# Four graph layers on one core: halves for the first and last group, a 64x64 turn of the adjacency, and later places for its forms and for the layernorms of layer 2

## The chip, the cores and the metric

The kernel runs on one core of a Trainium2 chip. A core has five engines that take their instructions in order, each from its own queue: TensorE (PE, with its weight loads shown apart as PEld), VectorE (DVE), ScalarE (ACT), GpSimd (POOL) and SyncE (SP), which only issues DMAs here. The metric is the device time of one execution in microseconds (us). The version before takes 2535.03 us, the median of three runs from 2534.58 to 2535.87. All values are fp32.

## The reference

x holds 128 batches of 64 nodes with 256 features; adj is one 64x64 matrix for all batches. There are four layers, each with a layernorm and a ReLU in front and a residual add behind.

```python
# layer 0: two graph convolutions, then LSTMs over windows of 1 to 4 nodes
h = relu(einsum('ts,bsh->bth', adj, x @ Wg0 + bg0))
h = relu(einsum('ts,bsh->bth', adj, h @ Wg1 + bg1))
for p in range(1, 5):
    ...
# layer 1: attention with 4 heads, masked where adj == 0
# layer 2: normalized adjacency and a net with two batchnorms
A_norm = A + eye(n)
deg = sum(A_norm, 0) + sum(A_norm, 1) - diagonal(A_norm)
dinv = rsqrt(deg)
A_hat = A_norm * dinv[:, None] * dinv[None, :]
x = einsum('nm,bmd->bnd', A_hat, features).reshape(-1, d)
h = relu(batchnorm(x @ W1.T + b1))
out = batchnorm(h @ W2.T + b2)
# layer 3: three times support = x @ W, then (adj * adj) @ support, with ReLU after the first two
# around each of them:
h = maximum(layernorm(x), 0.0)
x = x + layer(h)
```

The adjacency is thus needed in several forms: transposed for the graph convolution (`adj2`), its row sums for the biases, squared (`w2s`), as a mask, and normalized with both degrees (`ah2`).

## The kernel before, in words

The 8192 tokens (128 batches x 64 nodes) are worked in NG = 16 groups of GN = 512 tokens. A group is four tiles (GT) of 128 tokens on the partitions, two batches in a tile, so the adjacency stands twice on the partitions, once for each half of 64. All results of TensorE go through eight PSUM banks in rotation (`bank`). The order of the instructions on each engine comes from a scheduler; `tc.issue_after(ins)` tells it to put what follows behind `ins`. An engine stands still at an instruction whose input isn't ready, whatever is behind it.

Helpers: `ln_scale` (L83 to L98) makes the scale and shift of a layernorm for four tiles: four bn_stats on DVE (L91), four bn_aggr (L93), an add (L94), a power of -0.5 on POOL (L95) and a product on DVE (L97). `ln_apply` (L102) is four ACT activations, one for each tile. `mix` (L122 to L147) multiplies the tokens with a 64x64 adjacency form in 64 small matmuls (L134) into two banks and copies the two banks to SBUF (L146, in layer 3 also L143), by the engines that it is given. `seven` (L153 to L180) combines seven products to a 2x2 block product, with adds on DVE (L165, L166, L174, L177) and POOL (L169), and hands its blocks to `ends_in` (L197), which puts the ReLU of layer 3 on ACT, from a bank (L202) for the first block and in place (L204) for the other three.

Layer 0: the adjacency arrives twice from memory on ACT's queue. `abd` (L270) holds it as two 64x64 blocks on the diagonal of a cleared 128x128 tile, `arow` (L272) holds it in two stacks of rows. One 128x128 transpose turns `abd` (L275), and two 64x64 copies (L280) put the diagonal blocks in `adj2`; they are called from within the layernorm of group 0, ahead of L97. `adjacency_forms` (L285 to L300) makes the row sums by a matmul (L290), the mask, `w2s` and a full copy of the turned tile; `normalized_adjacency` (L302 to L323) makes `ah2`, with degrees from three reductions, a power on POOL (L317), another 128x128 transpose (L320) and two products (L323). Both are called at group 1, behind its layernorm. The loop at L419 runs over g and calls in this order: `first_mix(g)`, `second_weights(g-2)` (L407, adds L412, ReLU on ACT L415), `second_mix(g-1)` with both copies on ACT, `first_weights(g)` (L383, adds L391 on DVE, ReLU L392 on POOL). The x tiles come by SP's queue (L58), the weights of the convolution by ACT's (L328).

Layer 2: `activated` (L664) is the layernorm of a group, `mixed` (L670) its mix with `ah2`, `hidden` (L674) sixteen matmuls into four banks (L680), each bank read by ACT (L686, the eviction with the bias) and by DVE (bn_stats, L689). The loop at L882 calls for each g the layernorm and the mix of g+1, then hidden(g). All layernorms there may start as soon as the attention is done (`after_attention`), as far as buffers and queues allow. After the first batchnorm (`bn_finish`, L862) the loop at L918 applies it (L921), multiplies with the second weight matrix, eight matmuls a group into two banks (L928), evicts the banks on ACT (L937) and then takes their statistics on DVE (L940). A second `bn_finish` follows; nothing of layer 3 can start before it.

Layer 3: `normalize` (L947) applies the second batchnorm, one feature half on ACT (L951) and one on DVE (L954). `to_residual` (L957) turns the result by eight transposes (L964) in two banks, and adds each bank to x (L968). `start` (L971) is the layernorm and first mix of a group, `first_weights` (L981, products L991) ends in the ReLUs of `ends_in`, `second_mix` (L1006) mixes them in two rounds, `second_weights` (L1027) and `third_weights` (L1072) follow, `last_mix` (L1093) is the last adjacency product, and `finish` (L1100) adds two banks to x (L1103) and sends 512 KB out (L1104).

Of the kernel before, what the change touches and what calls it, by code (L numbers as in the profile page):

```python
# [8 lines left out]
F32 = mybir.dt.float32  # L9
AF = mybir.ActivationFunctionType  # L10
# [4 lines left out]
P = 128  # L15
# [23 lines left out]
def adj_preln_kernel(ctx: ExitStack, tc: tile.TileContext, x_in, adj, vec, bg0, bg1,  # L39
# [31 lines left out]
    adjT = const.tile([P, P], F32, tag="adjT", name="adjT")  # L71
# [11 lines left out]
    def ln_scale(src, between=None):  # L83


        st = lnp.tile([P, GT, 6], F32, tag="st", name="st")
        mv = lnp.tile([P, GT, 2], F32, tag="mv", name="mv")
        rstd = lnp.tile([P, GT], F32, tag="rstd", name="rstd")
        nmr = lnp.tile([P, GT], F32, tag="nmr", name="nmr")
        for t in range(GT):  # L90
            nc.vector.bn_stats(st[:, t, :], src[:, t, :])  # L91
        for t in range(GT):
            nc.vector.bn_aggr(mv[:, t, :], st[:, t, :])  # L93
        nc.vector.tensor_scalar(rstd, mv[:, :, 1], LN_EPS, None, ALU.add)  # L94
        nc.gpsimd.tensor_tensor(out=rstd, in0=rstd, in1=mhalf, op=ALU.pow)  # L95
        with tc.issue_after(between().ins) if between else nullcontext():
            last = nc.vector.scalar_tensor_tensor(nmr, mv[:, :, 0], -1.0, rstd, ALU.mult, ALU.mult)  # L97
        return rstd, nmr, last.ins  # L98

    def ln_apply(src, dst, rstd, nmr):  # L100
        for t in range(GT):
            nc.scalar.activation(  # L102
                dst[:, t, :], src[:, t, :], AF.Relu,
                bias=nmr[:, t : t + 1], scale=rstd[:, t : t + 1],
            )
# [91 lines left out]
    def ends_in(out, func):  # L197


        def end(m, n, ps):  # L200
            if ps is not None:
                nc.scalar.activation(out[m][n], ps, func)  # L202
            elif func != AF.Copy:
                nc.scalar.activation(out[m][n], out[m][n], func)  # L204

        return end
# [45 lines left out]
    with tc.tile_pool(name="lw", bufs=5) as lw:  # L252
# [6 lines left out]
        with tc.tile_pool(name="gw", bufs=1) as gw, tc.tile_pool(name="gcn", bufs=2) as gp, \  # L259
                tc.tile_pool(name="setup", bufs=1) as sp:  # L260

            for g in range(2):
                load_x(xs[g], g)
            abd = sp.tile([P, P], F32, tag="abd", name="abd")
            nc.vector.memset(abd, 0.0)
            arow = sp.tile([P, NODES], F32, tag="arow", name="arow")
            ones = sp.tile([NODES, P], F32, tag="ones", name="ones")
            nc.vector.memset(ones, 1.0)
            for b in range(2):
                nc.scalar.dma_start(out=abd[b * 64 : b * 64 + 64, b * 64 : b * 64 + 64], in_=adj)  # L270
            for b in range(2):
                nc.scalar.dma_start(out=arow[b * 64 : b * 64 + 64, :], in_=adj)  # L272
            nc.sync.dma_start(out=vecs, in_=vec)
            pt = bank((P, P))
            nc.tensor.transpose(pt, abd, ident)  # L275

            def diagonal_blocks():
                for b in range(2):
                    blk = slice(b * 64, b * 64 + 64)
                    last = nc.vector.tensor_copy(adj2[blk, :], pt[blk, blk])  # L280
                return last

            rstd0, nmr0, first_ln = ln_scale(xs[0], diagonal_blocks)

            def adjacency_forms():  # L285
                nc.vector.tensor_tensor(
                    lbias, vecs[:, V_BIH : V_BIH + 32], vecs[:, V_BHH : V_BHH + 32], ALU.add
                )
# [5 lines left out]
                for c in range(2):  # L294
                    nc.vector.tensor_scalar(
                        rb1[:, c, 0, :], rsrow, bcol[:, c : c + 1], None, ALU.mult
                    )
                nc.vector.tensor_scalar(mask, arow, 0.0, NEG, ALU.is_equal, ALU.mult)
                nc.vector.tensor_tensor(w2s, adj2, adj2, ALU.mult)
                nc.vector.tensor_copy(adjT, pt)  # L300

            def normalized_adjacency():  # L302
                an = sp.tile([P, P], F32, tag="an", name="an")
                anT = sp.tile([P, P], F32, tag="anT", name="anT")
                dg = sp.tile([P, P], F32, tag="dg", name="dg")
# [3 lines left out]
                nc.vector.tensor_tensor(an, abd, ident, ALU.add)  # L309
                nc.vector.tensor_tensor(anT, adjT, ident, ALU.add)  # L310
                nc.vector.tensor_tensor(dg, an, ident, ALU.mult)
# [7 lines left out]
                pt2 = bank((P, P))  # L319
                nc.tensor.transpose(pt2, an, ident)  # L320
                for b in range(2):
                    blk = slice(b * 64, b * 64 + 64)
                    nc.vector.tensor_scalar(ah2[blk, :], pt2[blk, blk], dinv[blk, :], None, ALU.mult)  # L323
# [20 lines left out]
            first_copied, middle_copied, second_ln = None, None, None  # L344

            def first_mix(g):
                nonlocal first_copied, middle_copied, second_ln
                h = gp.tile([P, GT, D], F32, tag="h", name="h")
                if g == 0:
                    ln_apply(xs[0], h, rstd0, nmr0)  # L350
                elif g == 1:

                    with tc.issue_after(first_copied):
                        rstd, nmr, second_ln = ln_scale(xs[1])
                    ln_apply(xs[1], h, rstd, nmr)
                    with tc.issue_after(second_ln):
                        adjacency_forms()
                        normalized_adjacency()
                else:
# [5 lines left out]
                    with tc.issue_after(second_ln):  # L365
                        ln_relu(x, h)
                m0 = gp.tile([P, 2, GN], F32, tag="m0", name="m0")
                copied = mix(h, adj2, 2, m0, (on_vector, on_vector))
                if g == 0:
                    first_copied = copied  # L370
                if g == NG // 2:
                    middle_copied = copied
# [22 lines left out]
            def second_mix(h1):  # L395
                m1 = gp.tile([P, 2, GN], F32, tag="m1", name="m1")
                mix(h1, adj2, 2, m1, (on_scalar, on_scalar))
# [21 lines left out]
            for g in range(NG + 2):  # L419
# [4 lines left out]
                m1 = second_mix(h1) if h1 is not None else None  # L424
# [249 lines left out]
    def hidden(g, w1, ms=range(4)):  # L674
# [10 lines left out]
        for m, ps in zip(ms, pss):  # L685
# [3 lines left out]
            nc.vector.bn_stats(st1[:, m, g, :], ps)  # L689


    with tc.tile_pool(name="att", bufs=2, reuse_waits="tile") as ap_:
# [113 lines left out]
        for g in range(NG + 1):  # L806
# [31 lines left out]
            else:  # L838
                hidden(0, w1, range(2, 4))
# [41 lines left out]

    for g in range(1, NG):  # L882
        if g + 1 < NG:
            with tc.issue_after(after_attention):
# [3 lines left out]
        hidden(g, w1)  # L888
# [29 lines left out]
    for g in range(NG):  # L918
# [7 lines left out]
        for c in range(4):  # L926
            for m in range(2):
                nc.tensor.matmul(  # L928
                    pss[m], lhsT=w2[:, c, m * P : (m + 1) * P], rhs=a[:, c, :],
                    start=(c == 0), stop=(c == 3),  # L930
                )
# [4 lines left out]
        for m in range(2):  # L936
            nc.scalar.activation(  # L937
                o[:, m, :], pss[m], AF.Identity, bias=vecs[:, V_B2 + m : V_B2 + m + 1]
            )
            nc.vector.bn_stats(st2[:, m, g, :], pss[m])  # L940
# [6 lines left out]
    def normalize(g):  # L947

        o = outs[g // 2][:, 2 * (g % 2) : 2 * (g % 2) + 2, :]
# [7 lines left out]
    def to_residual(g):  # L957
        o = outs[g // 2][:, 2 * (g % 2) : 2 * (g % 2) + 2, :]
        for k in range(2):
# [11 lines left out]
    def start(g, behind=None):  # L971
# [4 lines left out]
        with tc.issue_after(behind) if behind else nullcontext():  # L976
            ln_relu(xs[g], h)
# [3 lines left out]
    def first_weights(a, room):  # L981
# [6 lines left out]
        def product(w, b):  # L988
# [13 lines left out]
            blocks, ends_in(blocks, AF.Relu),  # L1002
# [97 lines left out]
    def finish(g, pss):  # L1100
        for q in range(2):
# [21 lines left out]
    normalize(0)  # L1123
    to_residual(0)
    a = start(0)
# [77 lines left out]
```

## Time and profile before

| | us |
|---|---|
| median of three runs | 2535.03 |
| the profiled execution, its own time | 2534.2 |
| its span | 2532.4 |
| TensorE busy in it | 2481.1 |
| DVE busy | 1462.8 |
| ACT busy | 1132.3 |
| POOL busy | 418.5 |

The mean clock granted to TensorE is 0.993 of full speed. The profile is one execution; its times are microseconds from the start of the span. A timeline row gives start and duration, engine and line, operation, output and inputs, shape and count, and in brackets how long the engine was idle before it and what ended that. A row of waits gives the waiting engine and line, what it waited for, and then the total, the number of times and the longest. A row of windows gives for a stretch of time the busy time of each engine (with instructions begun), the granted clock, the DMA engines' busy share and GB/s.

Three rows of DMA issues, with the time from issue to landing at the end:

```profile
x<-in_x SPq DMA_DIRECT2D x28, 512.0 KB, 6.2
out<-x SPq DMA_DIRECT2D x16, 512.0 KB, 2.9
...
wg<-in_wg ACTq DMA_DIRECT2D x2, 256.0 KB, 4.0
```

The end of the execution, in the timeline:

```profile
2525.75 1.34 PE L1093 MATMUL ps<-arena,w2s 64*64 64x256 f32 x16
...
2527.13 1.29 DVE L1103 TENSOR_TENSOR x<-x,ps 128x512 f32<-128x512 f32 x2 [0.85 <-PE ps L1093]
2528.44 0.37 SPq L1104 DMA_DIRECT2D out<-x  x1
```

The last two adds begin when the last matmuls are done, and the span ends when the last 512 KB have been sent.

### The profile page before, as it was taken

What the parts mean: (1) busy time and instruction counts of PE and PEld (TensorE: products, weight loads), DVE (VectorE), ACT (ScalarE), POOL (GpSimd) and SP (SyncE); (2) the same over time, 40 slices, a digit from 0 to 9 for tenths busy, and PEclk for the clock granted to TensorE, in tenths of its full rate; (3) what the DMA queues carried; (4) which work ended last, traced back from release to release, by engine and by line L of the source; (5) the groups of instructions that cost most, each with busy time, mean ns of one, the idle gap of its engine ahead of it and who ended that gap; (6) DMA issues with size and microseconds to landing.
All of it is one profiled execution on the core that took longest, in us unless ns stands there. A gap on an engine that the chain in (4) does not pass through costs nothing.

```text
span 2532.4 us, 46818 instructions
## 1 busy us (share of the span) xinstructions
PE 2481.1 (98%) x20184; PEld 2046.5 (81%) x20184; DVE 1462.8 (58%) x2606; ACT 1132.3 (45%) x1982; POOL 418.5 (17%) x350
## 2 busy tenths in 40 slices
PE   7999999999999999999999989998999999999999
PEld 5668888889999998888766654445898888888888
DVE  6647876666566575565566675415455454554544
ACT  4547754444444443444555464653333333333332
POOL 3422211111111111111122220003101101111110
PEclk9999999999999999999999999998999999999999
DMA  3200000001000000000300000010000000000000
GB/s 113 102 1 1 1 17 1 1 1 34 1 1 1 1 1 1 1 13 1 101 2 2 2 19 1 1 58 1 9 10 10 18 10 10 18 10 10 18 9 18
DMA packets 30206, 39.66 MB, mean 16 GB/s; under 512 B 1712, under 2 KB 26416, under 8 KB 30000
## 3 DMA queue, kind: packets, MB, share of 16 engines
q1 hardware_dynamic: 29136, 36.09, 4.2%
q8 instruction: 158, 2.59, 0.4%
q10 hardware_dynamic: 864, 0.59, 0.1%
q14 instruction: 48, 0.39, 0.1%
HBM read 28.29 MB, written 8.39 MB: 14 GB/s over the span
## 4 chain that ended last, share of the span: by engine, by line
PE 90%; DVE 4%; ACT 2%; POOL 2%; issue 1%; DMA 0%; DVEq 0%; POOLq 0%; ACTq 0%
PE ps L461 40%; PE ps L1027 15%; PE ps L1072 8%; PE ps L707 4%; PE ps L928 4%; PE ps L134 4%; PE ps L680 3%; PE ps L991 3%; PE ps L723 2%; PE ps L383 2%; PE ps L407 2%; POOL rstd L95 1%; DVE st L91 1%; ACT arena L204 1%; PE ps L784 1%
## 5 line engine op out<-in xcount | busy, mean ns | idle before, releaser
L461 PE MATMUL ps<-diff,s 128*128 128x256 f32 (+1 forms) x1824 | 393.5, 371 | 0.9 <-DVE diff L577 0.9
L1027 PE MATMUL ps<-arena 128*128 128x256 f32 x1792 | 392.7, 381 | 0.8 <-DVE arena L186 0.8
L1027 PEld LDWEIGHTS ps<-arena 128*128 128x128 f32 x1792 | 337.8, 190 | 55.1 <-issue 10.4
L461 PEld LDWEIGHTS ps<-diff,s 128*128 128x128 f32 x1824 | 345.9, 190 | 33.8 <-issue 1.6
L475 ACT ACTIVATE gates<-gates,lbias 128x512 f32<-128x512 f32 (+5 forms) x426 | 244.1, 620 | 203.6 <-DVE gates L174 146.3
L169 POOL TENSOR_TENSOR gates<-p 128x512 f32<-128x512 f32 (+1 forms) x115 | 148.8, 1294 | 885.1 <-DVE p L166 834.0
L461 PE MATMUL ps<-h,w 128*128 128x256 f32 (+1 forms) x1028 | 241.2, 371 | 1.6 <-ACT p L162 1.6
L461 PE MATMUL ps<-diff,w 128*128 128x256 f32 (+1 forms) x1040 | 238.7, 370 | 0.0
L461 PEld LDWEIGHTS ps<-diff,w 128*128 128x128 f32 x1040 | 197.4, 190 | 18.2
L461 PEld LDWEIGHTS ps<-h,w 128*128 128x128 f32 x1028 | 194.6, 190 | 20.9 <-ACT p L162 2.0
L475 ACT ACTIVATE gates<-ps,lbias 128x256 f32<-128x256 f32 (+3 forms) x213 | 91.8, 477 | 247.0 <-PE ps L461 246.9
L204 ACT ACTIVATE arena<-arena 128x512 f32<-128x512 f32 x144 | 88.1, 628 | 192.4 <-POOL arena L169 103.3
L169 POOL TENSOR_TENSOR arena<-arena 128x512 f32<-128x512 f32 x64 | 73.2, 1144 | 537.9 <-DVE arena L166 537.9
L1072 PE MATMUL ps<-arena 128*128 128x128 f32 x1280 | 149.9, 276 | 0.0
L1072 PEld LDWEIGHTS ps<-arena 128*128 128x128 f32 x1280 | 145.6, 192 | 1.3 <-issue 0.2
L174 DVE TENSOR_TENSOR gates<-p,ps 128x512 f32<-128x512 f32 (+1 forms) x115 | 76.5, 665 | 119.8 <-PE ps L461 119.8
L174 DVE TENSOR_TENSOR arena<-arena,ps 128x512 f32<-128x512 f32 x64 | 39.7, 621 | 149.4 <-PE ps L1027 84.7
L680 PE MATMUL ps<-arena,w 128*128 128x512 f32 x256 | 115.8, 605 | 1.4 <-DVE arena L146 1.3
L461 PE MATMUL ps<-state,w 128*128 128x256 f32 (+1 forms) x512 | 116.1, 370 | 0.9 <-ACT p L162 0.8
L461 PE MATMUL ps<-state,s 128*128 128x256 f32 (+1 forms) x512 | 115.8, 369 | 0.0
L177 DVE TENSOR_TENSOR gates<-p,ps 128x512 f32<-128x512 f32 (+1 forms) x115 | 76.7, 667 | 64.8 <-PE ps L461 64.1
L707 PE MATMUL ps<-hT,w 128*128 128x512 f32 x256 | 112.8, 593 | 0.0
(184 smaller groups left out, 3884.2 us busy)
## 6 DMA issues: line engine op xcount, KB each, us to landing
x<-in_x SPq DMA_DIRECT2D x28, 512.0 KB, 6.2
out<-x SPq DMA_DIRECT2D x16, 512.0 KB, 2.9
w<-in_wih SPq DMA_DIRECT2D x4, 1024.0 KB, 7.6
w<-in_whh SPq DMA_DIRECT2D x3, 1024.0 KB, 5.0
arena<-in_l3w SPq DMA_DIRECT2D x3, 1024.0 KB, 5.0
w<-in_wqkv SPq DMA_DIRECT2D x1, 768.0 KB, 4.4
wg<-in_wg ACTq DMA_DIRECT2D x2, 256.0 KB, 4.0
w<-in_w1t SPq DMA_DIRECT2D x1, 512.0 KB, 3.8
```

The costliest lines, as they stand in the source:

```text
L134: nc.tensor.matmul(pss[b][half * 64 : half * 64 + 64, c, t, :], lhsT=src[rows, t, col : col + 64], rhs=a2[rows, :], start=True, stop=True,)
L169: nc.gpsimd.tensor_tensor(out=out[1][1], in0=p1, in1=p5, op=ALU.add)
L174: nc.vector.tensor_tensor(out[0][1], p1, ps[1], ALU.add)
L177: nc.vector.tensor_tensor(out[1][0], p1, ps[3], ALU.add)
L204: nc.scalar.activation(out[m][n], out[m][n], func)
L461: nc.tensor.matmul(ps[:, r], lhsT=wc[:, j, :], rhs=bc, start=first and r == 0 and c == 0, stop=True, skip_group_check=True,)
L475: nc.scalar.activation(o, ps, func, bias=lbias[:, col : col + 1])
L680: nc.tensor.matmul(ps, lhsT=w1[:, c, m * P : (m + 1) * P], rhs=a[:, 2 + c, :], start=(c == 0), stop=(c == 1),)
L707: nc.tensor.matmul(ps, lhsT=wqk[:, c, col : col + P], rhs=hT[:, c, :], start=(c == 0), stop=(c == 1),)
L928: nc.tensor.matmul(pss[m], lhsT=w2[:, c, m * P : (m + 1) * P], rhs=a[:, c, :], start=(c == 0), stop=(c == 3),)
L1027: nc.tensor.matmul(ps[:, r, :], lhsT=w[:, c, col : col + P], rhs=b[:, c, :], start=first and r == 0 and c == 0, stop=c == 1, skip_group_ch ...
L1072: nc.tensor.matmul(ps[:, t, :], lhsT=w[:, c, t * P : (t + 1) * P], rhs=b[:, c, :], start=first and t == 0 and c == 0, stop=c == 3, skip_gr ...
```

## The change

1. `abd`, its clearing, its two DMAs and `adjT` are gone. The adjacency is turned by two 64x64 matmuls of `arow` with the identity (`by_batch`), one for each half of the partitions, into one 128x64 bank, and one copy makes `adj2`. The DMAs of `arow` are the first on ACT's queue. x of group 0 is loaded in two halves, and its layernorm is made and applied in two halves of two tiles (`ln_scale` and `ln_apply` with n = 2).
2. Of group 0's mix the first bank is copied by ACT, the second by DVE. The layernorm of group 1 is put behind that of group 0, not behind the copies.
3. The row sums stay at group 1. The other forms and the normalized adjacency, now 128x64 each, are made at group NG // 4 = 4, behind the copies of its mix.
4. The second mix of the last group is copied by ACT and DVE.
5. In layer 2 the layernorm of group g+1 is put behind the statistics of hidden(g-3), for the first groups behind the attention and hidden(0).
6. In the second half of layer 2 the statistics of a bank are called ahead of its eviction, and the last group's eight matmuls fill one bank after the other.
7. Group 0 of layer 3 is normalized, turned, added, and put through its layernorm by halves.
8. Of the four ReLUs of a group in layer 3's first product, that of block (1, 0) is on DVE.
9. The last group is added in four parts and sent out in two halves.

```diff
-            abd = sp.tile([P, P], F32, tag="abd", name="abd")
-            nc.vector.memset(abd, 0.0)
-            for b in range(2):
-                nc.scalar.dma_start(out=abd[b * 64 : b * 64 + 64, b * 64 : b * 64 + 64], in_=adj)
+            for k in range(2):
+                nc.sync.dma_start(
+                    out=xs[0][:, 2 * k : 2 * k + 2, :], in_=x_view[:, 2 * k : 2 * k + 2, :]
+                )
...
-            pt = bank((P, P))
-            nc.tensor.transpose(pt, abd, ident)
+            def by_batch(ps, rows):
                 for b in range(2):
                     blk = slice(b * 64, b * 64 + 64)
-                    last = nc.vector.tensor_copy(adj2[blk, :], pt[blk, blk])
+                    nc.tensor.matmul(
+                        ps[blk, :], lhsT=rows[blk, :], rhs=ident[blk, blk], start=True, stop=True
+                    )
+            pt = bank((P, NODES))
+            by_batch(pt, arow)
+            lns = [
+                ln_scale(xs[0][:, 0:2], lambda: nc.vector.tensor_copy(adj2, pt), 2),
+                ln_scale(xs[0][:, 2:4], None, 2),
+            ]
+            first_ln = lns[1][2]
...
-                nc.vector.tensor_tensor(an, abd, ident, ALU.add)
-                nc.vector.tensor_tensor(anT, adjT, ident, ALU.add)
-                nc.vector.tensor_tensor(dg, an, ident, ALU.mult)
+                nc.vector.tensor_tensor(eye, ident[:, 0:64], ident[:, 64:128], ALU.add)
+                nc.vector.tensor_tensor(an, arow, eye, ALU.add)
+                nc.vector.tensor_tensor(anT, adj2, eye, ALU.add)
+                nc.vector.tensor_tensor(dg, an, eye, ALU.mult)
...
-                pt2 = bank((P, P))
-                nc.tensor.transpose(pt2, an, ident)
+                pt2 = bank((P, NODES))
+                by_batch(pt2, an)
+                nc.vector.tensor_scalar(ah2, pt2, dinv, None, ALU.mult)
...
-                    with tc.issue_after(first_copied):
-                        rstd, nmr, second_ln = ln_scale(xs[1])
-                    ln_apply(xs[1], h, rstd, nmr)
-                    with tc.issue_after(second_ln):
-                        adjacency_forms()
-                        normalized_adjacency()
+                    with tc.issue_after(first_ln):
+                        rstd, nmr, _ = ln_scale(xs[1])
+                    with tc.issue_after(first_scalar):
+                        ln_apply(xs[1], h, rstd, nmr)
+                    with tc.issue_after(first_copied):
+                        row_sums()
...
+                if g == NG // 4:
+                    with tc.issue_after(copied):
+                        adjacency_forms()
+                        normalized_adjacency()
...
-                mix(h1, adj2, 2, m1, (on_scalar, on_scalar))
+                mix(h1, adj2, 2, m1, (on_scalar, on_vector if last else on_scalar))
...
+    behind = [after_attention, after_attention, counted]
     for g in range(1, NG):
         if g + 1 < NG:
-            with tc.issue_after(after_attention):
+            with tc.issue_after(behind[g - 1]):
...
-        hidden(g, w1)
+        behind.append(hidden(g, w1))
...
+        order = [(c, m) for c in range(4) for m in range(2)]
+        if g == NG - 1:
+            order.sort(key=lambda cm: cm[1])
...
         for m in range(2):
+            nc.vector.bn_stats(st2[:, m, g, :], pss[m])
             nc.scalar.activation(
                 o[:, m, :], pss[m], AF.Identity, bias=vecs[:, V_B2 + m : V_B2 + m + 1]
             )
-            nc.vector.bn_stats(st2[:, m, g, :], pss[m])
...
+        if g == 0:
+            for k in range(2):
+                two = slice(2 * k, 2 * k + 2)
+                to_residual(0, [k])
+                rstd, nmr, _ = ln_scale(xs[0][:, two], None, 2)
+                ln_apply(xs[0][:, two], h[:, two], rstd, nmr, 2)
...
+            elif (m, n) in on_vector:
+                nc.vector.tensor_scalar(out[m][n], out[m][n], 0.0, None, ALU.max)
...
-            blocks, ends_in(blocks, AF.Relu),
+            blocks, ends_in(blocks, AF.Relu, [(1, 0)]),
...
+        if g == NG - 1:
+            for k in range(2):
+                for q in range(2):
+                    xt = xs[g][:, 2 * k + q, :]
+                    nc.vector.tensor_tensor(xt, xt, pss[q][:, k, :], ALU.add)
+                two = slice(2 * k, 2 * k + 2)
+                t0 = g * GT + 2 * k
+                nc.sync.dma_start(out=out_view[:, t0 : t0 + 2, :], in_=xs[g][:, two, :])
+            return
...
-    normalize(0)
-    to_residual(0)
-    a = start(0)
+    for k in range(2):
+        normalize(0, slice(k * HN, (k + 1) * HN))
+    a = start(0, None)
```

## The prediction, made before the changed kernel was run

> **What bounds the kernel.** I read the busy shares first, then the waits of TensorE, then the timeline at each wait, then windows that show the clock beside the busy time.
>
> ```profile
> span 2532.4 us, 46818 instructions
> PE 2481.1 (98%) x20184; PEld 2046.5 (81%) x20184; DVE 1462.8 (58%) x2606; ACT 1132.3 (45%) x1982; POOL 418.5 (17%) x350
> ```
>
> TensorE works in 98% of the span, so it is the bound; all that it stands idle for is 2532.4 - 2481.1 = 51.3 us. The change removes no large matmul, so it can win only what is in those 51 us and what a low clock adds behind a wait. The waits of TensorE (total, times, longest) say where they lie:
>
> ```profile
> PE ps L275 <- DMA abd<-in_adj: 6.9, 1, 6.9
> PE ps L134 <- DVE st L689: 5.0, 8, 1.7
> PE ps L134 <- ACT arena L102: 4.6, 1, 4.6
> PE ps L964 <- ACT arena L951: 4.5, 1, 4.5
> PE ps L383 <- DVE m L146: 4.0, 3, 1.9
> PE ps L320 <- DVE an L318: 3.5, 1, 3.5
> PE ps L134 <- ACT arena L204: 3.1, 12, 0.3
> ```
>
> The parts of the change touch these rows, and one further on at L407. The sum is made against the profiled execution: 2534.2 us, 1.8 over its span and 0.8 under the median of 2535.03.
>
> **Start of layer 0.** The timeline:
>
> ```profile
> 6.91 0.45 PE L275 MATMUL ps<-ident,abd 128*128 128x128 f32 x1 [6.91 <-DMA abd<-in_adj]
> 8.10 2.08 ACT L102 ACTIVATE h<-x,nmr,rstd 128x256 f32<-128x256 f32 x4 [1.96 <-DVE nmr L97]
> 12.97 5.66 PE L383 MATMUL ps<-wg,m 128*128 128x256 f32 x16 [1.39 <-DVE m L146]
> 22.45 0.33 PE L320 MATMUL ps<-ident,an 128*128 128x128 f32 x1 [3.46 <-DVE an L318]
> ```
>
> abd goes with two DMAs of ACT's queue and a memset, so arow is issued some 1.3 us earlier and lands near 5.6 to 6.5. The first half of the layernorm: stats 0.7 from 4.8 (half of the four in 1.41), two aggregations and the add 0.35, the pow 0.72 (estimate between the rows of 0.57 for one column and 1.01 for four), nmr 0.16: near 6.85. Four L102 at 0.50 end at 8.85 instead of 10.18. On SP's queue the halves of x0 add one issue (0.5), which x1 has time for (its stats ran at 12.83); on ACT's queue the weights of L383 go out 1.3 earlier. The mix ends 1.4 later, near 10.3. Its copies now go to ACT (0.59) and DVE (0.69) beside each other; but x1's layernorm stands ahead of the DVE copy now: rsum, stats 1.40, rb0, aggregations 0.36, the add 0.17, a wait for POOL's pow 1.01, nmr, which ends near 11.3. So L383 starts at about 12.1 to 12.4: gain 0.6 only. The larger gain is L320: it stood between L290 and the mix of group 1 and cost 3.46. With it gone, that mix starts when L383 ends, 12.4 + 5.66, at some 18.3 instead of 22.71. The next late thing is the POOL ReLU (L392, 1.5) of the second mix, as before. I follow the lead to the third group, where L383 ran at 49.76 and should at 45.75: **+4.0** (2 to 5.5; the low end if arow's second half or bg0 lands late). From 60 to 170 us TensorE is 100% busy, 9.48 us a group, so the lead is kept.
>
> **The forms at group 4, which speak against the change.** Their twelve DVE operations, pow and turn now stand behind the copies of mix 4, and on TensorE the two 64x64 products stand between mix 4 and L407 of group 2. TensorE is in order, so it stands still from the end of mix 4: two copies 1.29, the chain of small operations about 1.8 (spaced 0.07 to 0.20, as at 17.40 to 21.3), pow 0.58 and its hand-over 0.15, the product with dinv 0.2: 4.0 to 4.6, of which all is new, since L407's inputs are ready. **-4.3**. Behind it the clock falls. What that costs is seen at the end of the front, where the wait is shorter (windows: us, PE, PEld, DVE, ACT, POOL busy, PEclk):
>
> ```profile
> 173.66 5.40 PE L407 MATMUL ps<-m,wg 128*128 128x512 f32 x8 [1.82 <-ACT m L146]
> ```
> ```profile
> 173.00:174.00 1.00, 0.34 (x1) 0.30 (x2) 0.00 (x0) 0.61 (x2) 0.00 (x0) 0.97 0.00 0
> 174.00:175.00 1.00, 1.00 (x2) 0.34 (x1) 0.00 (x0) 0.00 (x0) 0.00 (x0) 0.50 0.00 0
> 177.00:178.00 1.00, 1.00 (x3) 0.53 (x2) 0.68 (x1) 0.00 (x0) 0.00 (x0) 0.83 0.00 0
> ```
>
> Half clock from 174.0 to 177.4, and L407 took 5.40 instead of 3.63: 1.77 lost. After 4.3 us of idling the low stretch may begin inside the wait or run two windows long (1.7 to 3.4): I take **-2.5**. The part is **-6.8** (-4 to -8). The cover, if there were any, would be other matmuls queued ahead; there are none.
>
> **End of the front.** The last second mix has its copies on ACT and DVE instead of both on ACT: the wait of 1.82 shrinks by one ACT copy less the DVE excess, 0.5. Here a rule and the row differ. The Trainium skill, page "TensorE: Matmul & The Clock Gate", section "What's actually happening", says that the clock halves after an idle window of about 3.4 us. By that rule a 1.8 us wait costs nothing beyond itself and the edit is worth 0.5; by the row the 1.82 us wait was followed by 3.4 us of half clock, so if 1.3 us escapes it the edit is worth 2.3. I can't tell where the limit lies, and take **+1.2** (0.5 to 2.3). For group 4 both say that the clock falls.
>
> **Layer 2.**
>
> ```profile
> 1500.00:1520.00 20.00, 16.45 (x158) 8.05 (x157) 16.39 (x64) 15.20 (x29) 5.74 (x6) 0.97 0.00 1
> 1520.00:1540.00 20.00, 17.18 (x141) 7.73 (x144) 13.80 (x51) 15.85 (x30) 4.32 (x5) 0.95 0.00 0
> ```
>
> With all layernorms let go at once behind the attention, DVE and ACT are crowded in these 40 us and TensorE loses 6.4; afterwards it is full, at 7.03 (sixteen L680) + 1.13 (mix) = 8.16 a cycle. From 1497.93 to 1597.67 eleven cycles would take 89.8, so 9.9 is lost there, 1.7 of it as half clock (one L680 group took 8.83, not 7.13). The change ties layernorm g+1 to the statistics of hidden g-3, which leaves one in each cycle. Nothing is then early, and the engines close a loop. ACT, in order, runs eviction, two L102, eviction, two L102, two evictions: from nmr to the last one 3.80 (four L102 at 0.50, three evictions at 0.57 to 0.69). Then the last statistics 0.63, three stats of the next layernorm 1.01, two copies 1.19, and the last stat, aggregations, add, pow 1.01 and nmr 2.25: 8.9, which is over 8.16. The scheme starts with some 2.8 us in hand, so the excess of 0.72 over ten cycles leaves TensorE late by 7.2 - 2.8 = 4.4 less what the last layernorms, which aren't there, give back (1.0): 3.4. **+6.5** (9.9 if the loop stays below 8.16; 3 at 9.25; each 0.1 of the loop is worth 1.0).
>
> **From layer 2 to layer 3.**
>
> ```profile
> 1735.41 1.97 PE L964 MATMUL ps<-ident,arena 128*128 128x128 f32 x8 [4.52 <-ACT arena L951]
> 1741.94 2.82 PE L134 MATMUL ps<-w2s,arena 64*64 64x64 f32 x64 [4.56 <-ACT arena L102]
> ```
>
> The last group's eight L928 go bank by bank, so one bank is full 3.4 us early and its statistics and parameters are done under the other's matmuls; the statistics (0.70) now also stand ahead of the eviction (0.69) instead of behind it. Left of 4.52 are statistics 0.7, aggregation 0.6, seven small ones 0.6, pow 0.57 and half of L951 0.5: 3.1, **+1.4**. The halved layernorm starts its stats one L968 add earlier (0.69), but pays a second pow (0.72 instead of nothing) on the way: **+0.45**. Together **+1.85** (1.2 to 3.5, the high end if the clock no longer falls).
>
> **ReLU on DVE.** L134 waits 12 times for the last of three ACT ReLUs, 0.26 each. One of the three (0.58) moves to DVE, directly behind L177 in eleven groups. DVE then ends it at about L177 + 0.55, some 0.2 before the old moment: 11 x 0.2 = **+2.2** (0.5 to 2.9). In groups 0 to 4 it stands behind an L968 add of 0.69: nothing either way.
>
> **Finish.** The last two adds took 1.29 and wait for the last product, and so do the four half-width ones (0.42 each). The first half DMA leaves 0.85 behind the start instead of 1.3, and the last is 256 KB instead of 512 (2.9 to landing): **+0.5** (0 to 1.1).
>
> **Sum.** 4.0 - 6.8 + 1.2 + 6.5 + 1.85 + 2.2 + 0.5 = 9.45: 2534.2 - 9.5 = 2524.7 profiled, and with the 0.8 to the median **2525.5**.
>
> **Rivals.** A measurement tells from no change about 0.2%, 5 us.
> - *The larger gain* (chance 0.25): the layer-2 loop doesn't bind (9.9) and the stop at group 4 costs only itself, 4.3: 2525.5 - 3.4 - 2.5 = 2519.6. For it: the loop is only 9% above TensorE's own time. Against: 1.82 us already cost the clock.
> - *Within 0.2%* (0.15): the stop at group 4 costs 8, the lead is 3, and the loop is 9.25: 2534.2 - (3 - 8 + 1.2 + 3 + 1.5 + 1.5 + 0.3) = 2531.7, or 2532.5 at the median.
> - *Slower* (0.03): the layer-2 loop takes 10.4 a cycle, for instance if each statistics reading of a bank holds ACT's eviction back (5 x 0.3), or pow waits for POOL; (10.4 - 8.9) x 10 = 15 more, 2540.5. The whole turns slower from about 9.8 to 9.9 a cycle. Against: crowded as they were, DVE and ACT let one group take 11.1 us at worst (1507.57 to 1518.70), with three layernorms in that time (six POOL operations in the first of the two windows).
> - The likeliest keeps 0.57. That the scheduler undoes the delay isn't likely: the order of DVE's queue has one layernorm in each cycle.
>
> Range: 2519 to 2531, from the larger gain to the stop at 8 with a loop of 9.2. Faster 0.82, same 0.15, slower 0.03.
>
> **What would show it.** L383 of group 1 near 23.4; the 64x64 products at group 4 with a wait of 4 to 4.6 and L407 behind them above 5; L680 of groups 10 and up each behind a wait of about 0.7 on a mix that waits for L102; L964 with a wait of 3.1; no L204 row among the waits. Wrong would be: no wait at group 4, layer-2 waits of 2 us and more, or a lead that is gone by 60 us.

## The result, and the profile after

The changed kernel takes 2528.33 us (median of 11 runs, 2527.07 to 2532.12) against 2535.03 us (11 runs): the ratio is 0.9977 with an interval of 0.9968 to 0.9986. That is 6.7 us less. Forecast were 2525.5 and a gain of 9.5, in a range of 2519 to 2531.

The page of the profile after, first the span, then the busy time of each engine:

```profile
span 2530.3 us, 46856 instructions
...
PE 2478.1 (98%) x20190; PEld 2044.8 (81%) x20190; DVE 1469.4 (58%) x2626; ACT 1119.3 (44%) x1967; POOL 419.4 (17%) x352
```

This execution took 2532.1 us, 3.8 over the median of its kernel, so its span shows only 2.1 of the gain. A second profile of the same kernel (after_again below) was of an execution of 2528.3. Both are used here.

The waits of TensorE after the change (engine, line waited at, what it waited for; total, times, longest):

```profile
PE ps L280 <- DVE an L327: 5.8, 1, 5.8
PE ps L280 <- DMA arow<-in_adj: 5.0, 2, 3.9
PE ps L406 <- ACT h L101: 4.7, 1, 4.7
PE ps L703 <- DVE arena L145: 4.7, 7, 0.7
PE ps L133 <- DVE arena L204: 4.6, 11, 0.4
PE ps L133 <- ACT arena L101: 4.0, 1, 4.0
PE ps L406 <- DVE m L145: 2.7, 2, 2.0
...
PE ps L133 <- issue: 2.3, 1, 2.3
PE ps L993 <- ACT arena L980: 2.0, 1, 2.0
...
PE ps L430 <- ACT m L145: 1.3, 1, 1.3
...
PE ps L993 <- DVE arena L983: 1.0, 1, 1.0
```

Line numbers have moved: L406 is the old L383, L430 the old L407, L703 the old L680, L957 the old L928, L993 the old L964, L1130 the old L1093. Two rows of before are gone: that of L320 (3.5) and the waits of layer 2's mixes for statistics (5.0). Two are shorter: the wait for the adjacency at the start (6.9, now 5.0) and that in front of layer 3 (4.5, now 2.0 and 1.0). New are 5.8 us at the 64x64 products of group 4 (L280, L327), seven waits of up to 0.7 in layer 2, and eleven of 0.4 for the ReLU on DVE, where twelve for ACT's (3.1 in all) stood before.

Where the time went is read from the start of one instruction at the end of each stage, in three profiles. A gain is how much a stage shortened:

| up to the start of | before | after | after_again | gain in after_again |
|---|---|---|---|---|
| L383 / L406 of group 3 | 49.76 | 47.42 | 46.42 | +3.3 |
| the second mix behind L407 / L430 of group 2 | 58.14 | 64.90 | 63.49 | -8.7 |
| first LSTM matmul | 178.90 | 183.41 | 182.03 | +2.2 |
| hidden(1) of layer 2 | 1489.78 | 1496.27 | 1493.02 | -0.1 |
| first L928 / L957 | 1619.59 | 1621.33 | 1618.13 | +4.7 |
| first mix of layer 3 | 1741.94 | 1741.09 | 1738.51 | +2.0 |
| last L1093 / L1130 | 2525.75 | 2524.12 | 2520.32 | +2.0 |
| end of the span | 2532.4 | 2530.3 | 2526.5 | +0.5 |

The gains add up to 5.9, as the spans do (2532.4 - 2526.5). One stage loses more than any other gains.

### The profile page after: what moved, and what is told of

Its sections match the earlier page's. It is cut to its first block, busy times and chain, and to the rows that moved or that the text cites. A ratio compares the mean times of both kernels' runs of the same rounds, so it can differ in the third digit from the quotient of the medians.

```text
span 2530.3 us, 46856 instructions
## 1 busy us (share of the span) xinstructions
PE 2478.1 (98%) x20190; PEld 2044.8 (81%) x20190; DVE 1469.4 (58%) x2626; ACT 1119.3 (44%) x1967; POOL 419.4 (17%) x352
## 4 chain that ended last, share of the span: by engine, by line
PE 90%; DVE 5%; ACT 2%; issue 1%; POOL 1%; DMA 1%; POOLq 0%; DVEq 0%; ACTq 0%
PE ps L484 40%; PE ps L1064 15%; PE ps L1109 8%; PE ps L731 4%; PE ps L957 4%; PE ps L1028 4%; PE ps L133 3%; PE ps L747 2%; PE ps L406 2%; PE ps L430 2%; DVE st L90 1%; POOL rstd L94 1%; PE ps L703 1%; ACT arena L101 1%; DVE st L712 1%
## 5 line engine op out<-in xcount | busy, mean ns | idle before, releaser
L206 ACT ACTIVATE arena<-arena 128x512 f32<-128x512 f32 x128 | 78.7, 628 | 192.7 <-POOL arena L168 104.0
L173 DVE TENSOR_TENSOR gates<-p,ps 128x512 f32<-128x512 f32 (+1 forms) x115 | 76.4, 664 | 120.2 <-PE ps L484 120.2
L94 POOL TENSOR_TENSOR rstd<-rstd,mhalf 128x4 f32<-128x4 f32 (+1 forms) x66 | 66.7, 1010 | 338.5 <-DVE rstd L93 327.4
L703 PE MATMUL ps<-arena,w 128*128 128x512 f32 x256 | 115.2, 603 | 4.7 <-DVE arena L145 4.7
L101 ACT ACTIVATE arena<-x,nmr,rstd 128x256 f32<-128x256 f32 x128 | 67.7, 590 | 109.8 <-DVE nmr L96 104.4
```

The costliest lines, as they stand in the source:

```text
L94: nc.gpsimd.tensor_tensor(out=rstd, in0=rstd, in1=mhalf[:, 0:n], op=ALU.pow)
L101: nc.scalar.activation(dst[:, t, :], src[:, t, :], AF.Relu, bias=nmr[:, t : t + 1], scale=rstd[:, t : t + 1],)
L173: nc.vector.tensor_tensor(out[0][1], p1, ps[1], ALU.add)
L703: nc.tensor.matmul(ps, lhsT=w1[:, c, m * P : (m + 1) * P], rhs=a[:, 2 + c, :], start=(c == 0), stop=(c == 1),)
```

## The experiments

**after_again**, the changed kernel unaltered.

> The changed kernel unaltered, for a second profile beside the others. The first profile was of an execution of 2532.1, 3.8 over the median. Theory: the low clock behind the 2.3 us wait in front of the first mixes of layer 2 (L703 4.86 instead of 3.70) is chance of that execution, because the kernel before had the same schedule there with a wait of 1.8 and kept its clock; then this profile shows 1.1 to 2 us less there and a span near 2526. Rival: the low clock belongs to the changed kernel, and L703 shows 4.8 again.

Median 2527.85 us (7 runs). The row that differs is the first group of L703, behind a wait of 2.33 us in the first profile and of 1.93 in the second (timeline of TensorE, first of after, then of after_again):

```profile
1484.33 0.90 PE L133 MATMUL ps<-ah,arena 64*64 64x64 f32 x18 [2.33 <-issue]
1485.15 4.86 PE L703 MATMUL ps<-arena,w 128*128 128x512 f32 x8
```
```profile
1482.57 0.56 PE L133 MATMUL ps<-ah,arena 64*64 64x64 f32 x18 [1.93 <-issue]
1483.06 3.70 PE L703 MATMUL ps<-arena,w 128*128 128x512 f32 x8
```

The low clock there is not a property of the changed kernel. Five later profiles show it again, and two of them (before_l2 and before_relu) are of the kernel before with a single edit. The theory held, but not its reason, the length of the wait; see the last section.

**turn_late**: the forms stay at group 4, the two products and `ah2` come behind the mix of group 5.

```diff
-                pt2 = bank((P, NODES))
-                by_batch(pt2, an)
-                nc.vector.tensor_scalar(ah2, pt2, dinv, None, ALU.mult)
+                def turn():
+                    pt2 = bank((P, NODES))
+                    by_batch(pt2, an)
+                    nc.vector.tensor_scalar(ah2, pt2, dinv, None, ALU.mult)
+                return turn
...
+                if g == NG // 4 + 1:
+                    with tc.issue_after(copied):
+                        turn()
```

> The adjacency forms stay at group 4 on DVE and POOL, but the two 64x64 products and the product into ah2 come behind the mix of group 5, so that TensorE has L430 of group 2, the second mix and L406 between. Theory: the wait of 5.8 at L280 is gone and L430 takes 3.7 instead of 6.5, 8.5 to 9 us less. Rival: the chain of twelve DVE operations, 2.6 us long, delays the adds and ReLUs behind it, so that a wait of 2 to 4 comes back at the next mix; then 4 to 6 less.

Median 2521.61 us (4 runs, 2521.01 to 2521.96), 6.2 to 6.7 less than the changed kernel; 8.5 to 9 were expected. The first LSTM matmul starts at 173.96, against 182.03 in after_again: 8.1 earlier, and 8.7 if counted from L406 of group 3, so the stop itself was worth what was expected. Of the 8.1, 7.3 is left at the end of the span (2519.2 against 2526.5): the first sixteen products of layer 3 (L1028) took 6.58 in this profile and 5.13 in after_again, 1.45 more at a lower clock, in the same code. TensorE around the products, in after and then in turn_late (where L438 is L430):

```profile
51.08 1.16 PE L133 MATMUL ps<-adj,h 64*64 64x64 f32 x64
58.05 0.48 PE L280 MATMUL ps<-ident,an 64*64 64x64 f32 x4 [5.81 <-DVE an L327]
58.46 6.52 PE L430 MATMUL ps<-m,wg 128*128 128x512 f32 x8
```
```profile
61.11 0.30 PE L280 MATMUL ps<-ident,an 64*64 64x64 f32 x4
61.34 3.70 PE L438 MATMUL ps<-m,wg 128*128 128x512 f32 x8
```

The wait is gone and L430 has its warm time, with all twelve DVE operations still at group 4. So the loss came from TensorE's order and not from the work of the forms. The rival's wait at the next mix did not come. Why the wait was 5.8 and not 4.3 is seen on DVE in after:

```profile
49.19 1.41 DVE L90 BATCH_NORM_STATS2 st<-x 128x6 f32<-128x256 f32 x4 [1.99 <-DMA x<-in_x]
...
52.37 0.16 DVE L96 SCALAR_TENSOR_TENSOR nmr<-mv,rstd 128x4 f32<-128x4 f32 x1 [1.22 <-POOL rstd L94]
52.45 1.28 DVE L414 TENSOR_TENSOR h<-ps,rb 128x512 f32<-128x512 f32 x2
...
53.65 1.28 DVE L145 COPY m<-ps 128x512 f32<-128x512 f32 x2
```

Mix 4 was done at 52.24. Its copies stood behind two adds (L414), these behind a layernorm's last step, and that layernorm had waited 1.99 us for its x to land. The copies came 1.4 late: 1.4 + 1.28, then 2.0 up to the last small operation at 56.95, and 1.1 for pow, the product and the hand-overs make 5.8. The profile of copy_first (next) has the same stop without that delay. There the mix ends at 52.47, the copies follow at once, and the wait is 4.09:

```profile
52.52 1.29 DVE L145 COPY m<-ps 128x512 f32<-128x512 f32 x2 [0.31 <-PE ps L133]
```
```profile
56.55 0.48 PE L280 MATMUL ps<-ident,an 64*64 64x64 f32 x4 [4.09 <-DVE an L327]
```

L430 behind it still took 6.43.

**copy_first**: the layernorm of x1 behind group 0's copies again.

```diff
-                    with tc.issue_after(first_ln):
+                    with tc.issue_after(first_copied):
                         rstd, nmr, _ = ln_scale(xs[1])
```

> Only the order of DVE at the start is undone: the layernorm of x1 stands behind the copies of group 0 again, as in the kernel before. Theory (the DVE half of the copy was ready to start near 9.9 and stood behind x1's late landing and POOL's pow until 13.7): L406 of group 0 starts near 10.8 instead of 14.5, and the third group's L406 is 2.5 to 3.8 us earlier; the time falls by about 3. Rival (x1 lands at 9.4, so the second group's mix can't come earlier anyway and L406 of group 0 was hidden): L406 of group 0 moves but the third group's does not, and the time stays within 1 us.

Median 2527.25 us (6 runs, 2525.48 to 2528.67) beside 2527.85 for after_again, not told apart. The DVE half of group 0's copy had indeed stood still in after: the first bank was copied by ACT at 9.85, the second by DVE at 13.73, because x1 landed late and the pow of its layernorm came in between.

```profile
9.39 0.43 DVE L90 BATCH_NORM_STATS2 st<-x 128x6 f32<-128x256 f32 x1 [2.56 <-DMA x<-in_x]
9.85 0.59 ACT L381 COPY m<-ps 128x512 f32<-128x512 f32 x1 [1.45 <-PE ps L133]
...
13.73 0.68 DVE L145 COPY m<-ps 128x512 f32<-128x512 f32 x1
...
14.51 6.29 PE L406 MATMUL ps<-wg,m 128*128 128x256 f32 x16 [4.71 <-ACT h L101]
```

The wait is put down to ACT h there, which had ended at 8.40; the copy at 13.73 was the last to come. In copy_first L406 follows the start of its mix by 3.71 us (8.50 to 12.21) instead of 6.79 in after_again (6.95 to 13.74). But L406 of group 1 starts at 24.42 against 24.82, and that of group 3 at 47.65 against 46.42. What was won at the first is lost by then: the rival is right that it was covered. (Its mix also began 1.55 later, for the second half of `arow` landed only at 7.0.) The cover seems to be DVE's queue, where layernorms of three groups stand ahead of the copies of mix 1; L406 of group 1 waits 2.0 to 2.3 for these copies in every profile with the changed start but that of best2.

**best2** was made to test that cover; it is the version best1 (below) with group 1's two copies on ACT.

> best1 with the two copies of group 1's first mix on ACT. Theory (L414 of group 1 waits 2.0 for DVE, whose queue has layernorms ahead of the copies, while ACT is idle from 21.3 on): L414 of group 1 starts 2 earlier and the lead stays, 2 us less than best1. Rival (the loads of x set the pace from the fourth group on, and DVE waits for them): within 0.7 us of best1.

Median 2516.33 us (5 runs) against 2516.17 for best1: nothing. L414 of group 1 (the products of L406) starts at 24.40 without a wait and takes 3.72 instead of 5.12, yet a mix behind it waits for POOL, 2.92 us in one piece:

```profile
36.63 0.97 PE L133 MATMUL ps<-adj,h 64*64 64x64 f32 x48 [2.92 <-POOL h L423]
```

L414 of group 2 begins at 37.54 here and at 36.91 in best1. The second of DVE's adds for that ReLU (at 34.31) stood behind a layernorm's last step (34.23), which waited for a pow, which stood behind POOL's first ReLU. So the rival's size is right, but in this profile not its cause: it is not the loads of x, but the same layernorms in the queues of DVE and POOL at another of their victims. The profile is of an execution of 2518.57, 2.2 over the median of best2, so what takes the gain in the usual execution isn't shown.

**l2_deep**: the layernorms of layer 2 one group earlier, by one more `after_attention` at the head of `behind`.

> The layernorms of layer 2 are let go one group earlier (behind hidden(g-4) instead of hidden(g-3)). Theory (the loop's excess of 0.78 a cycle eats a fixed lag, and this adds a whole cycle of lag): the seven waits of 0.4 to 0.7 at L703 vanish, 4.5 us less. Rival (ACT and DVE are in order and the loop between them stays 8.94 long whatever layernorm is in it; TensorE runs into full banks once the lag is used up): the same period of 8.94 from the seventh or eighth group on, waits at L133 or L703 of the same sum, 0 to 1 us less.

Median 2529.77 us (12 runs), 1.4 to 1.9 more than the changed kernel instead of less. Its waits at L703 begin two groups sooner, at 1524.85 instead of 1545.71, are as long (0.71), and are eight instead of seven (5.4 in all, for 4.7). The loop has its own length, whichever layernorm is in it. In after, one turn of it on DVE and ACT (from nmr to the next nmr, 1565.56 to 1574.50):

```profile
1565.56 0.16 DVE L96 SCALAR_TENSOR_TENSOR nmr<-mv,rstd 128x4 f32<-128x4 f32 x1 [1.21 <-POOL rstd L94]
...
1569.01 1.30 DVE L712 BATCH_NORM_STATS2 st<-ps 128x6 f32<-128x512 f32 x2 [0.85 <-ACT arena L709]
...
1571.20 1.27 DVE L145 COPY arena<-ps 128x512 f32<-128x512 f32 x2
...
1574.50 0.16 DVE L96 SCALAR_TENSOR_TENSOR nmr<-mv,rstd 128x4 f32<-128x4 f32 x1 [1.21 <-POOL rstd L94]
```
```profile
1565.76 1.09 ACT L101 ACTIVATE arena<-x,nmr,rstd 128x256 f32<-128x256 f32 x2 [4.57 <-DVE nmr L96]
1566.76 0.67 ACT L709 ACTIVATE arena<-ps,vecs 128x512 f32<-128x512 f32 x1
1567.32 1.08 ACT L101 ACTIVATE arena<-x,nmr,rstd 128x256 f32<-128x256 f32 x2
1568.31 1.81 ACT L709 ACTIVATE arena<-ps,vecs 128x512 f32<-128x512 f32 x3
```

That is 8.94 us, and L703 of the groups at 1563.59 and 1572.53 is 8.94 apart. ACT is idle for 4.57 of them: the loop is a chain of hand-overs, no engine is full.

**l2_early** cuts that chain: the layernorm goes behind the second statistics of hidden(g-3) instead of the fourth.

```diff
+        counts = []
...
-            last = nc.vector.bn_stats(st1[:, m, g, :], ps)
-        return last.ins
+            last = nc.vector.bn_stats(st1[:, m, g, :], ps)
+            counts.append(last.ins)
+        return counts[min(1, len(counts) - 1)]
```

> The layernorm g+1 of layer 2 is let go behind the second statistics of hidden(g-3) instead of the fourth. The scheduler then puts ACT's four evictions in one piece and the four L101 behind them, and the aggregations beside the last two evictions. Theory (the 8.94 are a chain of evictions, statistics, layernorm and L101 in order; cut to two evictions 1.25, statistics 0.6, the layernorm's stats 1.4, aggregations and pow 1.8, L101 2.1, it is 7.2, under TensorE's 8.16): the seven waits at L703 are gone, 4.5 us less than the changed kernel. Rival (DVE itself has no room left in these cycles, or banks come free later because the layernorm's stats stand ahead of the last two statistics): waits of the same size at L133 for the statistics, and within 1 us.

Median 2523.39 us (4 runs, 2522.61 to 2524.76), 4.5 to 4.9 less than the changed kernel, as expected. No wait at L703 is left; its groups are 8.16 apart from hidden(1) to the end:

```profile
1565.38 7.13 PE L703 MATMUL ps<-arena,w 128*128 128x512 f32 x16
...
1573.54 7.13 PE L703 MATMUL ps<-arena,w 128*128 128x512 f32 x16
```

**before_l2**: the kernel before with the change's delay of the layernorms alone.

> The kernel before with the later layernorms of layer 2 alone. Theory (the layer gains 4.7 by itself: 9.9 lost before, about 5 lost to the loop of 8.94): 4.5 to 5 us less than the kernel before. Rival (part of the gain in the changed kernel's trace comes from its later entry into the layer): 2 to 3 us less.

Median 2528.43 us (9 runs) against 2534.40 (21 runs), ratio 0.9975 with an interval of 0.9965 to 0.9985, so 3.8 to 8.9 less. From hidden(1) to the first product of the second weights it takes 125.05 (1489.88 to 1614.93) where before took 129.81: 4.8, as the theory said; the medians differ by 6.0. This part alone is worth most of what the whole change brings.

**before_relu** and **relu_split**: the ReLU of block (1, 0) on DVE alone in the kernel before, and in the changed kernel only from group 5 on.

> The kernel before with the ReLU of block (1, 0) on DVE in all groups of layer 3. Theory: 0.20 less in each of eleven groups, 0.24 more in about five, 1.0 us less, to be read from the period in the trace (47.84 instead of 48.05 in the late groups, 49.2 instead of 48.95 in the early ones) rather than from the median. Rival: the early loss belongs to the halved start, and all 2.2 us come.

> The ReLU of block (1, 0) is on DVE only from group 5 of layer 3 on; groups 0 to 4 have it on ACT as in the kernel before. Theory (in groups 0 to 4 it stands behind an add of 0.68 and costs TensorE 0.24 a group): about 1.2 us less than the changed kernel, with L1130 of group 4 as early relative to the first mix as in the kernel before. Rival (the 0.24 comes from the halved start of group 0, not from the ReLU): no change.

Medians 2533.73 us against 2534.40 (ratio 0.9996, 0.9988 to 1.0004), and 2527.97 us (20 runs) beside 2527.85 and 2528.33 for the changed kernel: neither can be told from nothing by its time. The traces can tell it by the distance between the second L1093 / L1130 of one group and the next:

| | before | before_relu | after_again | relu_split |
|---|---|---|---|---|
| an early pair of groups, near 1910 | 48.95 | 49.19 | 49.19 | 48.95 |
| a late pair, near 2055 | 48.05 | 47.85 | 47.84 | 47.85 |

Late groups gain 0.20 each, early ones lose 0.24, and they lose it with or without the halved start, and not where ACT has the ReLU. In an early group (L204 is the ReLU on DVE; the last row is TensorE's mix, which took 2.04 before):

```profile
1858.33 0.68 DVE L997 TENSOR_TENSOR x<-x,ps 128x512 f32<-128x512 f32 x1
...
1858.92 0.42 DVE L204 TENSOR_SCALAR arena<-arena 128x512 f32<-128x512 f32 x1
1858.97 2.29 PE L133 MATMUL ps<-w2s,arena 64*64 64x64 f32 x128
```

The ReLU comes one add later than it could, and TensorE pays a part of that add. In a late group TensorE goes on with the mix behind the same ReLUs, before and then after:

```profile
2006.08 1.74 PE L134 MATMUL ps<-w2s,arena 64*64 64x64 f32 x104 [0.27 <-ACT arena L204]
```
```profile
2006.49 1.86 PE L133 MATMUL ps<-w2s,arena 64*64 64x64 f32 x112 [0.41 <-DVE arena L204]
```

The wait in brackets is longer, but it ends 1.31 after the start of L1130 (2005.18) where it ended 1.51 after that of L1093 (2004.57): 0.20 sooner. The 1.2 us expected of relu_split in the time did not show; the trace has it in the periods only.

**end_scalar**: the last second mix copied by ACT alone again.

> The last second mix of layer 0 is copied by ACT alone again, the rest is the changed kernel. Theory (a wait of 1.8 in front of the last L430 costs half a clock window, as in the profile of the kernel before): the wait is 1.8 instead of 1.34 and L430 takes 5 to 5.4 instead of 3.70; 2 us more. Rival (in the waits of 1.9 to 2.3 in front of layer 2 the clock fell in one of five profiles, so it is chance): L430 takes 3.7, 0.5 us more.

Median 2529.08 us (17 runs), 0.8 to 1.2 over the changed kernel, between the rival's 0.5 and the theory's 2. The wait is 1.83 and L430 takes 3.70:

```profile
178.72 3.70 PE L430 MATMUL ps<-m,wg 128*128 128x512 f32 x8 [1.83 <-ACT m L145]
```

In this profile the rival was right, and two profiles of kernels with before's code there agree (1.82 and then 3.70 in before_relu and before_l2). The 5.40 of the first profile was that execution's.

**best1**: turn_late, relu_split and l2_early together.

> The late turn, the split ReLU and the early layernorms of layer 2 together. If the three are independent: 6.7 + 1.2 + 4.5 less than the changed kernel, about 2515.5. Rival (gains given back further on, as 0.8 of the late turn's 8.1 seems to be): 2518 to 2520.

Median 2516.17 us (4 runs, 2515.17 to 2516.56), ratio to before 0.9929 with an interval of 0.9913 to 0.9946: 18 us less than before, 12 less than the changed kernel. The three are independent within what can be measured.

## Why the prediction was right in sum, and where its steps were off

The direction and the range held, and the trace shows the stop at group 4, the low clock behind it and the loop of layer 2 that were named. The gain was 6.7 instead of 9.5. The steps at group 4, in layer 2 and at the ReLU were tested by runs of their own; those at the start, between layers 2 and 3 and at the finish are read from the traces alone. By its steps, with after_again:

- **Start of layer 0: +4.0 forecast, +3.3 measured.** The half layernorm and the freed L320 came as said. L406 was to start at 12.1 to 12.4 and started at 13.7 (after_again) and 14.5 (after), that of group 1 near 23.4 and started at 24.8: I had x1's stats begin once nmr was done, while x1 landed at 9.2 to 9.4 only. In copy_first, without this lateness, the lead at group 3 was no larger.
- **The forms at group 4: -6.8 forecast, -8.7 measured; the step that failed most, and a size.** "TensorE stands still from the end of mix 4: two copies 1.29 ..." took it that DVE would copy at once. It was 1.4 late for adds behind a layernorm that waited for its x; where DVE was free, in copy_first, the wait was 4.09, as reckoned. The low clock cost 2.4 and 2.8 (L430 6.14 and 6.52 for 3.70) where 2.5 was taken; it lasted 6.83 us, two of the windows of the last section, in all seven profiles that have the products at group 4. turn_late showed the cause.
- **End of the front: +1.2 forecast, 0.8 to 1.2 by end_scalar.** The table shows +2.2, but 1.70 of it is the low clock of the first profile before (L407 5.40 for 3.70; the prediction's 1.77 took 3.63 for it), which the other profiles of that code don't have. The shorter wait is worth 0.5; the rest in end_scalar's time would be executions whose clock falls there, which no profile of it shows.
- **Layer 2: +6.5 forecast, +4.7 measured.** The loop was put at 8.9 and is 8.94. What failed is its last term: "less what the last layernorms, which aren't there, give back (1.0)". Thirteen cycles took 111.2 (1496.27 to 1607.49) where 106.0 is TensorE's own time, 5.2 lost and not 3.4. From 1545.71 on only the last cycle ran at 8.16, and since that is TensorE's own pace, such a cycle gives nothing back. This term is 1.0 of the 1.8; the rest is not split further. l2_deep spoke for the loop and against a lag as the cause, l2_early removed it.
- **Layer 2 to layer 3: +1.85 forecast, +2.0 measured** (2.6 in the first profile). The wait at L993 is 2.0, and a second of 1.0 for DVE's half of the normalization, together 3.0 for the 3.1 forecast (its terms, 0.7, 0.6, 0.6, 0.57 and 0.5, add up to 2.97). The second part, +0.45, came out at 0.5 (4.56 became 4.0), but partly by luck: 0.69 less 0.72 isn't 0.45, and the statistics did not start "one L968 add earlier", for both adds still run ahead of them (L997 at 1736.54, twice; statistics at 1737.74). What is shorter there are the two statistics instead of four and the pow of two columns, 0.70 for 1.01.
- **ReLU on DVE: +2.2 forecast, about +1.0 real.** Late groups: 0.20 each, as said. "In groups 0 to 4 it stands behind an L968 add of 0.69: nothing either way" is the step that failed; it costs 0.24 in each. The sign "no L204 row among the waits" did not come either: the row grew from 3.1 to 4.6, though in late groups the wait ends 0.20 sooner. That the stage shows +2.0 in one profile and +0.8 in the other is the clock at its start: the first sixteen products took 6.32 before, 6.43 after and 5.13 in after_again.
- **Finish: +0.5 forecast, +0.5 measured.**

Without the low clock of the first profile before at the end of the front (1.7) and at the start of layer 3 (1.2), the table's 5.9 is only about 3. So the sum came nearer than its steps did, by chance as far as the clock is chance. The clock favours the changed kernel on average too: it was 0.9932 in the mean of the 21 executions before and 0.9948 in 18 of the changed kernel, and 0.0016 of 2530 us are 4.0 us. That is an estimate and an upper bound, since half clock in a wait costs nothing. How much of it the change earns by its shorter waits isn't separated here.

The rivals "larger gain" and "slower" fell: the loop did bind, and it never came near the 9.8 us at which the sum would have turned. The rival "within 0.2%" had the right ingredients, a stop of 8 and more and a smaller gain in layer 2. The measured gain, 0.23% by the ratio, lies just beyond that bound, and its interval (0.14% to 0.32%) has the bound in it.

## What to carry to other kernels

Before work is moved "to a later, quieter place", look at what stands right behind its last instruction on the engine that is the bound: the twelve small operations cost nothing at group 4, but two small products (0.4 us) one group too early in TensorE's queue cost 8. When a delay makes two in-order engines feed each other, add up one turn of the loop: to let the work go one cycle earlier left it at 8.94, to let it go in the middle of a cycle instead of at its end gave TensorE back its own 8.16. An operation that is moved to an idle engine pays for what stands ahead of it in that queue, and that may differ from group to group.

## What the runs showed of the hardware that had not been expected

The clock of TensorE falls after waits of about 2 us in some executions and not in others, at the same place in the same code. In front of the first mixes of layer 2, thirteen profiles have a wait of 1.77 to 2.47 us. In seven (1.77, 1.82, 1.91, 1.93, 2.07, 2.13 and 2.21) the eight matmuls behind it took 3.70; in six (1.93, 1.93, 2.10, 2.21, 2.33 and 2.47) they took 4.86 to 6.49. At the end of the front, 1.82 or 1.83 was followed by 3.70 three times and by 5.40 once. The lengths overlap, so the length alone doesn't decide.

What decides can be read from the clock in the same traces. In each trace the granted clock changes between 1.00 and 0.50 only, and at moments that lie whole multiples of 3.413 us apart. Each trace thus has a grid of windows, and the grid falls on other places of the program each time. The Trainium skill, page "TensorE: Matmul & The Clock Gate", section "What's actually happening", says that the window of about 3.4 us in which activity is counted runs freely and isn't started by the kernel; the grids agree. Laid on them, the thirteen waits come apart. Four of the thirteen:

| | the wait | most of it in one window | clock behind it |
|---|---|---|---|
| after_again | 1.93 | 1.68 | full |
| best1 | 1.93 | 1.93 | half |
| copy_first | 2.21 | 1.78 | full |
| best2 | 2.21 | 2.21 | half |

In all six with half clock 1.93 to 2.21 us lie in one window, in all seven with full clock 1.29 to 1.78. The window with the wait and the next one, in after_again and then in best1 (rows of windows; the granted clock, 1.00 or 0.50, is the third number from the end):

```profile
1478.90:1482.31 3.41, 1.74 (x110) 1.60 (x102) 3.29 (x4) 1.84 (x4) 0.00 (x0) 1.00 0.41 144
1482.31:1485.72 3.41, 3.15 (x24) 1.67 (x25) 3.41 (x7) 2.60 (x4) 2.29 (x2) 1.00 0.02 5
```
```profile
1471.77:1475.18 3.41, 1.48 (x59) 1.18 (x50) 3.34 (x5) 1.52 (x3) 0.02 (x1) 1.00 0.06 18
1475.18:1478.59 3.41, 3.41 (x5) 1.35 (x4) 2.48 (x5) 1.69 (x4) 2.48 (x2) 0.50 0.02 5
```

Counted over all windows at full clock in the thirteen traces: where TensorE had no matmul for 1.95 us or more of the 3.41, the next window was at half clock each time (48 of 48). Below 1.5 us it never was (0 of 9372), and between the two in 7 of 29. So the rule that the prediction quotes, a whole idle window, asks for too much, and the row that it set against it, 1.82 us, lies where both happen: of the three waits of 1.82 at the end of the front, each whole in one window, one was followed by half clock. No run moved a wait on purpose against the windows; the executions differ in it by chance.

It follows that one profile of a wait of 2 us is no measure of what the clock costs behind it. The times carry this chance: of the 21 executions before, those with a mean clock of 0.994 took 2532.7 to 2534.4 us, and those with 0.992 took 2535.7 to 2536.6.
